# Layer 0's cross-attention: one copy of keys and queries out of PSUM by ScalarE, their two variants made by GpSimd from the copy

## The chip, the core and the metric

The kernel runs on one core of a Trainium2 chip. A core has five engines that run at the same time, each through its own queue in order: TensorE (PE, with its weight loads shown as PEld), VectorE (DVE), ScalarE (ACT), GpSimd (POOL) and SyncE (SP, which here only starts transfers). Matrix products land in PSUM, whose eight banks TensorE fills and VectorE and ScalarE read; GpSimd works in SBUF here. The metric is the time of one execution on the device in microseconds.

## What is computed

A decoder of two layers on 32 sequences of 100 tokens, width 256, each layer with self-attention, cross-attention to a context of 361 rows of width 128, and a mixture of experts. Only layer 0's cross-attention is touched:

```python
x = x + _L0_xattn_ref(_layernorm(x, axis=-1), ctx_512, L0_xattn_Wq, L0_xattn_Wkv, L0_xattn_Wo)
...
Q = (x @ Wq.T).reshape(B, xN, NUM_HEADS, HEAD_DIM)          # 16 heads of 16
KV = (z @ Wkv.T).reshape(B, zN, 2, NUM_HEADS, HEAD_DIM)
attn = jnp.einsum('bqhd,bkhd->bhqk', Q, K) * SCALE          # SCALE = 1/4
attn = jax.nn.softmax(attn, axis=-1)
O = jnp.einsum('bhqk,bkhd->bqhd', attn, V).reshape(B, xN, DIM)
return O @ Wo.T
```

## The kernel before

All of it is float32. The stage `l0_xattn` treats one sequence b in two halves c of eight heads. A projection for half c puts eight heads of 16 on 128 partitions, so that 32 partitions hold two heads, an even one (j = 0) and an odd one (j = 1). Products are made on blocks of 32 partitions, four at once; to compute the scores of one head of a block, the other head's 16 rows have to be taken out. So queries and keys are stored in two variants. `queries` (L548) projects four sequences at a time into one bank and ScalarE writes the bank to SBUF twice (L555), each time scaled per partition by `quarter`, which is 1/4 on the rows of head j and 0 on the others. `keys` (L557) does one sequence at a time: ScalarE writes it twice (L562), scaled by `own` (1 on the rows of head j, else 0) with `one` added, a single row of ones among the foreign rows. That row of ones is multiplied by the negative maximum of the scores, which `maxima` places beside the queries, so that the second, turned product already has the maximum subtracted and ScalarE can apply the exponential directly.

The loop runs over steps M = 2b + c, 64 of them and two to drain. In a step TensorE does, in an order written out by hand (`manual_schedule`): the transposes of the maxima of M-1; the scores of (M, j = 0), whose maxima VectorE takes (L590); the turned scores of (M-1, 0), whose exponentials ScalarE takes (L612); the values of M-2; the scores and turned scores for j = 1; and then the extras: `keys` for the next sequence, `queries` of the next four sequences in the odd steps 2b+1 with b mod 4 of 0 or 1, the output projection of a finished tile of 128 rows in even steps, and `vals` (L575, ScalarE copies). All banks come from one ring of eight (`bank_t`; the tag "r" falls back to it), so TensorE can run ahead of the readers by eight banks at most.

The output path of a step: ScalarE copies the values' bank (L626), VectorE swaps the halves of each 32 rows (L627), GpSimd masks (L629) and adds (L631), a step later VectorE inverts the sums (L636, held back behind the first four maxima of its step), and GpSimd multiplies into `zT` (L640), which the output projection (`out_proj`) reads. The projection in step 2b needs the product that is made in that same step.

At the start of the stage GpSimd fills the value, key and maxima buffers (L527 to L535) and makes a few index rows (L537, L539). The queues of VectorE, ScalarE and GpSimd hold their instructions in about the order in which the code above emits them. The value buffers and three key buffers are used in turn; the query tile has two buffers.

Of the kernel before, what the change touches and what calls it, by code (L numbers as in the profile page):

```python
# [9 lines left out]
F32 = mybir.dt.float32  # L10
I32 = mybir.dt.int32
U32 = mybir.dt.uint32
AF = mybir.ActivationFunctionType
ALU = mybir.AluOpType
AX = mybir.AxisListType

P = 128
NB = 32
T = 100
# [5 lines left out]
L = 361  # L25
# [96 lines left out]
class Kernel:  # L122
# [355 lines left out]
    def l0_xattn(self):  # L478
        nc, tc, a = self.nc, self.tc, self.a
        with ExitStack() as st:  # L480
# [14 lines left out]
            for h in range(H):  # L495
# [4 lines left out]
            pool = st.enter_context(tc.tile_pool(name="p0x", bufs=2))  # L500
# [11 lines left out]
            own, quarter, one = (  # L512
                cp.tile([P, 2], F32, tag=n, name=n) for n in ("own", "quarter", "one")
            )
# [13 lines left out]
            for t in vs:  # L528
                t = t.rearrange("p c (h j) e -> p c h j e", j=2)
# [18 lines left out]
            def queries(b0, c):  # L548
                if c == 0:
                    q[b0 // 4] = pool.tile([P, 2, 2, 4 * T], F32, tag="qT", name="qT")  # L550
                pm = self.bank_t()[:, : 4 * T]
                self.mm(pm, [(wq[:, k, c * P : (c + 1) * P], self.xn_of(k, b0, 4)) for k in range(NK)])
                t = q[b0 // 4]
                for j in range(2):
                    nc.scalar.activation(t[:, c, j, :], pm, AF.Copy, scale=quarter[:, j : j + 1])  # L555

            def keys(b, c):  # L557
                pm = self.bank_t()[:, :L]
                self.mm(pm, [(wk[:, c * P : (c + 1) * P], ctx[b][:, :L])])
                t = ks[b % 3]  # L560
                for j in range(2):
                    nc.scalar.activation(  # L562
                        t[:, c, j, :L], pm, AF.Identity, bias=one[:, j : j + 1], scale=own[:, j : j + 1]
                    )

            def vals(b, c0, n):
# [92 lines left out]
            def extras(b):  # L659

                k0, k1, v0, v1, o, x = [None] * 6
                if b + 1 < NB:
                    k0, k1 = (lambda: keys(b + 1, 0)), (lambda: keys(b + 1, 1))
                    v0, v1 = (lambda: vals(b + 1, 0, 2)), (lambda: vals(b + 1, 2, 1))
                if b > 1 and tile_of(b - 2) is not None:
                    o = lambda: out(tile_of(b - 2))
                b0, i = b // 4 * 4, b % 4
                if i < 2 and b0 + 4 < NB:
                    x = lambda: queries(b0 + 4, i)
                return k0, v0, o, k1, v1, x  # L670
# [11 lines left out]
            with tc.manual_schedule(engines={mybir.EngineType.PE}):  # L682
                load(0)
                load(1)
                for c in range(2):
                    queries(0, c)
                for c in range(2):
                    keys(0, c)
# [3 lines left out]
                for M in range(last + 2):  # L692
                    b, c = divmod(M, 2)
# [1526 lines left out]
```

## Time and profile before

| | us |
|---|---|
| median of 3 runs (2873.34 to 2880.9) | 2878.42 |
| profiled execution, as timed | 2879.42 |
| its span in the profile | 2877.0 |
| layer 0's cross-attention, in the span | about 521 to 1000 |
| one step of its loop | about 7.15 |
| L562, key variants by ScalarE, 128 of 128x361 | 0.679 each |
| L555, query variants by ScalarE, 32 of 128x400 | 0.598 each |
| L612, exponentials, 512 of 121x300 | 0.426 each |
| L590, maxima by VectorE, 512 of 100x361 | 0.524 each |

Busy time of an engine is the union of its instructions, so two that overlap count once; a pair of L562 takes 1.22 us from the first start to the last end. A wait "A <- B" is idle time of A that ended when B was done. "PEld" waiting means that a weight load stood still, which stops TensorE only when the matmuls already under way run out. GpSimd's durations in a profile are rough; where two instructions follow each other the distance of their starts is the better reading.

### The profile page before, as it was taken

Reading aid. Unit: us, or ns where it says so; the run is one execution under the profiler, and the core shown is the slowest. Engines: PE = TensorE matmul, PEld = TensorE weight load, DVE = VectorE, ACT = ScalarE, POOL = GpSimd, SP = SyncE. Lnnn points to the kernel's source line nnn. Section 1 sums busy time; section 2 is a strip of 40 time slices with the busy share of each in tenths; the row PEclk is TensorE's granted clock in tenths of the full one; section 3 lists DMA queues with packets and bytes.
Section 4 is the critical chain, followed back from the end, with each engine's and each line's share of the span. In section 5 each row is a group of like instructions: output and inputs, shape, how many; then the busy total and the mean of one; then the engine's idle time right before and its main releaser. Section 6 shows DMA issues by size and latency. Waiting matters only on the chain. (4 is left out here: it accounts for less than half of the span.)

```text
span 2877.0 us, 64265 instructions
## 1 busy us (share of the span) xinstructions
PE 2757.1 (96%) x24856; PEld 2132.5 (74%) x24856; DVE 1768.6 (61%) x5173; ACT 1391.3 (48%) x4210; POOL 765.2 (27%) x960
## 2 busy tenths in 40 slices
PE   8999999999999899999999999999999999999892
PEld 7888888777777657888885777777777777776572
DVE  7666766687888732222226877767676666676453
ACT  5555655677767511222223226556656566566120
POOL 3222212332222253222211330020211312223473
PEclk9999999999999899999999999999999999999996
DMA  7444333000000033655553210010000000000496
GB/s 241 137 131 165 133 140 120 22 16 16 16 16 16 17 123 121 218 203 192 195 199 93 75 39 9 7 55 17 17 15 9 15 9 14 11 10 5 121 216 188
DMA packets 133870, 241.89 MB, mean 84 GB/s; under 512 B 40715, under 2 KB 105926, under 8 KB 126769
## 3 DMA queue, kind: packets, MB, share of 16 engines
q1 hardware_dynamic: 103488, 143.53, 16.1%
q0 software_dynamic: 26784, 90.83, 9.8%
q8 instruction: 201, 3.29, 0.5%
q10 hardware_dynamic: 3280, 3.28, 0.3%
q14 instruction: 117, 0.95, 0.1%
HBM read 152.12 MB, written 111.18 MB: 92 GB/s over the span
## 5 line engine op out<-in xcount | busy, mean ns | idle before, releaser
L1816 POOL DMA_INDIRECT x_d<-xr,slot x200 | 195.0, 975 | 670.6 <-ACT eT L844 590.9
L178 PE MATMUL ps_t<-xnT,wA 128*128 128x200 f32 (+1 forms) x1608 | 323.5, 348 | 2.3 <-DMA wA<-in_wq 1.6
L178 PE MATMUL ps_t<-cT,q 128*128 128x361 f32 (+1 forms) x832 | 306.5, 471 | 0.0
L844 ACT COPY eT<-ps_t 124x384 f32<-124x384 f32 x400 | 191.2, 486 | 225.3 <-PE ps_t L843 220.2
L178 PEld LDWEIGHTS ps_t<-xnT,wA 128*128 128x128 f32 x1608 | 273.9, 192 | 31.1 <-issue 15.5
L834 ACT ACTIVATE wBx<-ps_t,m 128x361 f32<-128x361 f32 x400 | 227.4, 569 | 119.5 <-DVE m L831 109.8
L178 PE MATMUL ps_t<-xT,w 128*128 128x256 f32 (+1 forms) x1276 | 260.2, 363 | 0.7 <-ACT xT L172 0.7
L590 DVE TENSOR_REDUCE m<-ps_t 100x1 f32<-100x361 f32 x512 | 239.7, 524 | 19.2 <-PE ps_t L178 19.1
L178 PEld LDWEIGHTS ps_t<-xT,w 128*128 128x128 f32 x1276 | 223.6, 190 | 36.2 <-issue 9.3
L831 DVE TENSOR_REDUCE m<-ps_t 128x1 f32<-128x361 f32 x400 | 210.7, 527 | 59.8 <-PE ps_t L178 57.5
L843 PEld LDWEIGHTS ps_t<-ident,wBx 128*124 128x124 f32 x1200 | 150.2, 139 | 117.7 <-issue 70.7
L612 ACT ACTIVATE e<-ps_t 121x300 f32<-121x300 f32 x512 | 173.9, 426 | 122.5 <-PE ps_t L178 122.4
L384 ACT ACTIVATE e<-s,m 100x100 f32<-100x100 f32 x512 | 185.6, 364 | 66.2 <-DVE m L378 66.2
L843 PE MATMUL ps_t<-ident,wBx 128*124 128x128 f32 x1200 | 196.7, 275 | 3.6 <-DVE top L1756 2.3
L178 PE MATMUL ps_t<-wA,cT 128*124 128x512 f32 x384 | 195.6, 597 | 0.0
L388 POOL TENSOR_TENSOR e<-e,rz 100x400 f32<-100x400 f32 x128 | 109.3, 854 | 323.8 <-PE ps_t L178 208.0
L1463 DVE TENSOR_TENSOR h<-ps_t,g 128x256 f32<-128x256 f32 (+1 forms) x145 | 58.2, 402 | 188.4 <-ACT g L1462 176.0
L836 DVE TENSOR_SCALAR wBx<-wBx,sums 128x361 f32<-128x361 f32 x400 | 165.6, 414 | 9.4
L178 PEld LDWEIGHTS ps_t<-q,k 32*121 32x121 f32 x3072 | 128.3, 181 | 33.3 <-issue 7.1
L855 PEld LDWEIGHTS ps_t<-eT,v 124*64 124x64 f32 x3072 | 135.8, 138 | 15.1 <-issue 7.4
L1462 ACT ACTIVATE g<-ps_t 128x256 f32<-128x256 f32 (+1 forms) x145 | 52.9, 365 | 190.9 <-PE ps_t L178 164.2
L855 PE MATMUL ps_t<-eT,v 124*64 124x100 f32 x3072 | 140.6, 251 | 0.8 <-issue 0.7
(334 smaller groups left out, 5415.8 us busy)
## 6 DMA issues: line engine op xcount, KB each, us to landing
x_d<-fill SPq DMA_DIRECT2D x16, 1284.0 KB
we<-in_wexp SPq DMA_DIRECT2D x32, 384.0 KB
cT<-in_ctxT SPq DMA_DIRECT2D x64, 186.0 KB
xe_d<-zero SPq DMA_DIRECT2D x8, 1028.0 KB
xe<-x_d SPq DMA_DIRECT2D x24, 321.0 KB
sum<-fill SPq DMA_DIRECT2D x10, 640.0 KB
yk<-y_d SPq DMA_DIRECT2D x25, 256.0 KB
xe<-xe_d SPq DMA_DIRECT2D x24, 257.0 KB
```

What stands on the lines that cost most here:

```text
L178: self.nc.tensor.matmul(out, lhsT=l, rhs=r, start=(i == 0), stop=(i == n - 1))
L384: nc.scalar.activation(t[:, i, :], s[:, i, :], AF.Exp, bias=m[:, i : i + 1], accum_out=rz[:, i : i + 1])
L388: nc.gpsimd.tensor_tensor(t[:, h, :], t[:, h, :], self.last(rz[:, h], T), ALU.mult)
L590: got = nc.vector.tensor_reduce(m[:, j, o : o + 1], ps[r], AX.X, ALU.max, negate=True)
L612: nc.scalar.activation(t[:, r], ps[r].rearrange("p (c t) -> p c t", c=NKC), AF.Exp)
L831: self.after = nc.vector.tensor_reduce(m, ps, AX.X, ALU.max, negate=True)
L834: nc.scalar.activation(t, ps, AF.Exp, bias=m, accum_out=z)
L836: nc.vector.tensor_scalar(t, t, z, None, ALU.mult)
L843: nc.tensor.transpose(pt[:, c, :], es[n % 5][:, c * KC : (c + 1) * KC], self.ident)
L844: self.after = nc.scalar.copy(eT[:, :, o : o + P], pt)
L855: nc.tensor.matmul(pz[64 * j : 64 * j + 64, i, :], lhsT=v[:, c, h * 64 : (h + 1) * 64], rhs=eT[:, c, o : o + T], start=(c == 0), stop=(c = ...
L1816: got = nc.gpsimd.indirect_dma_start(out=self.x1_d[:, :], out_offset=bass.IndirectOffsetOnAxis(ap=slot[:, j, k : k + 1], axis=0), in_=xr[: ...
```

## The change

`queries` and `keys` take one more tile, `raw`, with three buffers. ScalarE copies the bank into it once, with no scale and no bias, and GpSimd makes both variants from it with `tensor_scalar`: one operation (multiply) for queries, two (multiply, add) for keys. What is stored in the variants is the same.

```diff
             def queries(b0, c):
...
                 t = q[b0 // 4]
+                raw = pool.tile([P, 4 * T], F32, tag="raw", name="raw", bufs=3)
+                nc.scalar.copy(raw, pm)
                 for j in range(2):
-                    nc.scalar.activation(t[:, c, j, :], pm, AF.Copy, scale=quarter[:, j : j + 1])
+                    nc.gpsimd.tensor_scalar(t[:, c, j, :], raw, quarter[:, j : j + 1], None, ALU.mult)
 
             def keys(b, c):
...
                 t = ks[b % 3]
+                raw = pool.tile([P, 4 * T], F32, tag="raw", name="raw", bufs=3)[:, :L]
+                nc.scalar.copy(raw, pm)
                 for j in range(2):
-                    nc.scalar.activation(
-                        t[:, c, j, :L], pm, AF.Identity, bias=one[:, j : j + 1], scale=own[:, j : j + 1]
+                    nc.gpsimd.tensor_scalar(
+                        t[:, c, j, :L], raw, own[:, j : j + 1], one[:, j : j + 1], ALU.mult, ALU.add
                     )
```

The order of TensorE, the loads, the buffers of the variants and everything outside these two functions stay as they are.

## The prediction

> **What bounds the kernel now.** I read the page's engine totals first, then a table of busy time for the stage that the change touches, then the waits inside it, then the rows that can price the new instructions, and last the timeline at two places. The page:
>
> ```profile
> PE 2757.1 (96%) x24856; PEld 2132.5 (74%) x24856; DVE 1768.6 (61%) x5173; ACT 1391.3 (48%) x4210; POOL 765.2 (27%) x960
> ```
>
> The cross-attention of layer 0 runs from about 521 to 1000 us. Its busy table (stretch, length, then busy us of PE, PEld, DVE, ACT, POOL, then the granted clock):
>
> ```profile
> 521.00:540.00 19.00, 18.52 (x134) 11.22 (x138) 11.11 (x34) 13.65 (x36) 7.84 (x24) 1.00 0.15 42
> 540.00:980.00 440.00, 429.67 (x7547) 330.30 (x7547) 356.64 (x970) 309.94 (x897) 128.46 (x228) 1.00 0.06 15
> 980.00:1000.00 20.00, 14.44 (x258) 11.30 (x251) 11.07 (x41) 7.79 (x21) 6.69 (x12) 0.81 0.01 2
> ```
>
> TensorE is busy 429.67 of 440 us at full clock: it is the bound, and ScalarE (310) and VectorE (357) matter only where TensorE waits for them. GpSimd idles for 70%. The waits between 540 and 980 us (who <- whom: us, times, longest):
>
> ```profile
> POOL zT L640 <- DVE zd L636: 246.1, 52, 6.9
> ...
> PEld ps_t L178 <- DVE m L590: 19.6, 85, 0.8
> ...
> PEld ps_t L178 <- ACT v L575: 7.2, 12, 1.1
> ...
> PEld ps_t L178 <- ACT k L562: 4.3, 13, 0.4
> PEld ps_t L178 <- ACT e L612: 3.3, 5, 0.9
> PEld ps_t L178 <- ACT qT L555: 2.9, 9, 0.3
> ```
>
> The reader sees two things. ScalarE holds up the weight loads for 17.7 us (19.3 with 0.8 us each of matmul waits for L575 and L612). And the largest wait of all is harmless today: GpSimd, strictly in order, stands some 5 us in every step for VectorE's reciprocal. That idle time is the room the new work must fit into.
>
> **The prices.** Removed on ScalarE: 128 activations of L562 at 679 ns and 32 of L555 at 598 ns, 106 us. Added there: 64 copies of 128x361 and 16 of 128x400; the nearest rows are copies out of PSUM of 124x384 (L844, 486 ns) and 128x400 (L409, 492 ns), so 39 us. ScalarE loses 67 us.
>
> Added on GpSimd: 128 tensor_scalars of 128x361 with two operations and 32 of 128x400 with one. The rows:
>
> ```profile
> L629 POOL TENSOR_TENSOR zs<-zs,both 128x400 f32<-128x400 f32 x64 | 66.1, 1032 | 28.9 <-DVE zs L627 28.7
> L231 POOL TENSOR_SCALAR xnx<-x_sb,mv,rstd 128x256 f32<-128x256 f32 x18 | 21.8, 1218 | 47.2 <-DVE rstd L228 36.4 <-issue 10.8
> ```
>
> L231 is the same instruction as the keys': two per-partition operands, two operations. The timeline shows it in pairs of 2.46 us, so the duration is also the spacing. Two-operand GpSimd work grows from 199 ns at 4 columns to 397 at 100 (L640): 2.06 ns a column on some 190 ns. With that start, L231 grows by (1218 - 190)/256 = 4.0 ns a column. Keys: 190 + 361x4.0 = 1.64 us. Queries: the same rate gives 1.80 us; with one operation they may cost only what two-operand work does, 190 + 400x2.06 = 1.02 us. I take 1.80, from the row with the same operation, and keep 1.02 (and 0.94 for keys at the same rate) for the low end. GpSimd gains 128x1.64 + 32x1.80 = 268 us, from 143 to 411 of the 479 us.
>
> The Trainium skill (GPSIMD Engine Reference, Engine selection) says one-input elementwise work on GpSimd runs at roughly line rate. L231 contradicts it: at its clock of 1.2 GHz 256 columns would take some 0.2 us, not 1.22. By the rule (an estimate: about 0.5 us each) the first term below would be +5, the third 0, and the sum about -9; the measurement decides.
>
> **First term, the start of the stage.** GpSimd's queue:
>
> ```profile
> 521.09 4.16 POOL L527 MEMSET v<- 121x1536 f32 x3
> ...
> 528.67 0.23 POOL L539 COPY wAn<-ids 128x25 f32<-128x25 f32 x1
> ```
>
> and TensorE's first scores:
>
> ```profile
> 526.71 1.46 PE L178 MATMUL ps_t<-k,qT 32*100 32x361 f32 x10
> ```
>
> The memsets ahead end at 528.9. Behind them now stand four query variants, then the first key variant, which the first scores need: 528.9 + 4x1.80 + 1.64 = 537.7, against 526.71. TensorE has nothing else in its hand-written order: **+11 us**. At the low prices 533.9, +7. The fourth raw tile waits for the first (three buffers) and the value copies stand behind it on ScalarE; they are needed after the scores, so that costs nothing more.
>
> **Second term, relief.** Key and query banks come free after 0.5 us instead of 1.2, and the value copies queued behind start earlier. Of the 19.3 us the waits on L562, L555 and L575 can go (15.2); those on the exps stay. Bounds 0 (the next wait, for the maxima of L590, takes over) and -19. I take **-14**, since the removed instructions are themselves what is waited for.
>
> **Third term, GpSimd's queue.** ScalarE now makes raw tiles, GpSimd waits for each, and behind a waiting or running tensor_scalar stand the three products of the output path (L629, L631, L640). L640 releases TensorE's output projection in the same step. One odd step with queries and the step behind it:
>
> ```profile
> 646.46 1.36 ACT L612 ACTIVATE e<-ps_t 121x300 f32<-121x300 f32 x4 [0.99 <-PE ps_t L178]
> ...
> 653.08 0.54 POOL L640 TENSOR_TENSOR zT<-zd 128x68 f32<-128x68 f32 x2 [4.93 <-DVE zd L636]
> ```
>
> ```profile
> 654.28 0.83 PEld L178 LDWEIGHTS ps_t<-wB,zT 128*128 128x128 f32 x4 [0.20 <-issue]
> ```
>
> After the exps the raw key copy ends near 648.3. Without queries the two key variants end at 651.6, ahead of 653.08, when the reciprocal releases L640: hidden in the 4.93 us. With queries they end at 648.3 + 2x1.64 + 2x1.80 = 655.2, L640 ends at 655.7, and the projection loads at 655.8 instead of 654.28: 1.5 us. Queries stand in 14 odd steps of the loop; in 11 of the steps that follow there is a projection: **+16 us**. Bounds: 0 at the low prices (they end at 652.2), and +30 if every such delay also makes the next reciprocal late. That reciprocal runs a step later; its product then ends some 2 us late against a slack of about as much, so I count none. The variants are needed one step (about 7 us) after they are made: no wait for scores in the loop. Loads on SyncE do not move.
>
> VectorE gets no new work. The Trainium skill (SBUF — State Buffer, Who interferes with whom) says that a VectorE instruction with two SBUF inputs contends with GpSimd's reads. L1366 shows it elsewhere (444/479/946 ns min/median/max); in this stage the 20 instructions of L1540 stayed at 164/166/177 with GpSimd at 30%. By the rule (an estimate: 50 such small instructions, half a 1.6 us product each) 40 us of VectorE's time would go, against its 83 idle; I add nothing.
>
> **Sum.** 11 - 14 + 16 = +13. The profiled execution took 2879.42 us (span 2877.0 and 2.4 around it), 1 us above the median of the three runs shown: 2892.
>
> **Rivals.**
> GpSimd is cheaper (faster). If one variant costs about 1.0 us, the start is +7, the third term 0, relief -14 to -19: 2867 to 2873, and up to 2880 if relief is half. It decides from where the four variants together take less than 5.4 us (653.08 plus the projection's 0.66 us of slack), 1.36 each; L629 and L640 speak for it in general, L231, the only long tensor_scalar on this engine, against. 0.32.
> GpSimd becomes the bound. Eight steps last 57 us and hold 8x2.2 us of products now, plus 16 key and 4 query variants; above (57 - 17.6)/20 = 1.97 us each it is full. At 2.15, 3.6 us more per eight steps, eight times, is 29 us in place of 16 + some, with a start of +12: 2910 and above. Against: 1.64 and 1.80 leave 10%. 0.10.
> Relief is nothing. The weight loads freed of ScalarE wait for L590 instead, which already stops them 85 times: 11 + 16 = +27, 2906. Against: the 12 waits on L575 reach 1.1 us, too long for L590's 0.8. 0.08.
> The forecast, 2883 to 2901, has 0.50.
>
> **How the numbers follow.** About 0.3%, 8.6 us, is what a measurement of this kernel can tell: faster is below 2870, slower above 2887. The forecast gives 0.40 slower and 0.10 same; the cheap rival 0.18 faster and 0.14 same; the other two 0.18 slower. Range: 2868 to 2910, which leaves out the cheap rival's edge and the full-queue case; the likeliest case alone has 2883 to 2901.
>
> **What would show it.** First scores near 537 rather than 527; TENSOR_SCALAR rows on POOL at 1.6 and 1.8 us; GpSimd near 85% of the stage; waits of TensorE on zT L640 of 10 us or more, on the value copies near none; ScalarE 67 us less. Variants near 1.0 us, or no wait on zT, would prove the third term wrong; waits on k or qT inside the loop would mean a delay I left out.

## The result and the profile after

The changed kernel takes 2885.17 us (median of 7 runs, 2884.41 to 2887.89) against 2879.53 us (7 runs) before. The medians differ by 5.6 us; the ratio worked out from all the runs is 1.0027, with a 95% interval of 1.0018 to 1.0036, thus 5 to 10 us slower, at the edge of what can be told apart. The forecast was 2892 in a range of 2868 to 2910, slower. The direction holds; most of the working does not. The page's first line of busy time, after:

```profile
PE 2753.7 (95%) x24856; PEld 2131.5 (74%) x24856; DVE 1769.5 (61%) x5173; ACT 1338.8 (46%) x4130; POOL 887.5 (31%) x1120
```

ScalarE lost 52 us of busy time (1391.3 to 1338.8), not 67: the forecast added up single durations, but a pair of L562 overlaps and is busy for 1.22 us, not 1.36. GpSimd gained 122 (765.2 to 887.5), not 268. GpSimd's groups between 515 and 1010 us say why (line, tiles, shape, count, busy us, mean ns, idle before):

```profile
L566 POOL TENSOR_SCALAR k<-raw,own,one 128x361 f32<-128x361 f32 x128 | 81.4, 646 | 20.5 <-ACT raw L564 17.2
L633 POOL TENSOR_TENSOR zs<-zs,both 128x400 f32<-128x400 f32 x64 | 66.1, 1032 | 15.9 <-DVE zs L631 15.7
L557 POOL TENSOR_SCALAR qT<-raw,quarter 128x400 f32<-128x400 f32 x32 | 41.2, 1296 | 0.2
```

A key variant, with two operations on 361 columns, takes 0.65 us; a query variant, with one on 400 columns, takes 1.30. The row the price was taken from (L231, two operations, 1.22 us for 256 columns) holds for neither.

**Where the time went.** The time lost stands at the start of the stage. GpSimd's timeline there, then TensorE's:

```profile
527.98 0.18 POOL L535 MEMSET k<- 128x8 f32 x3
528.10 0.16 POOL L537 IOTA ids<- 128x25 f32 x1
528.25 1.29 POOL L557 TENSOR_SCALAR qT<-raw,quarter 128x400 f32<-128x400 f32 x1
529.50 0.22 POOL L539 COPY wAn<-ids 128x25 f32<-128x25 f32 x1
529.68 3.79 POOL L557 TENSOR_SCALAR qT<-raw,quarter 128x400 f32<-128x400 f32 x3
533.47 2.52 POOL L566 TENSOR_SCALAR k<-raw,own,one 128x361 f32<-128x361 f32 x4
```

```profile
534.16 2.74 PE L178 MATMUL ps_t<-k,qT 32*100 32x361 f32 x16 [7.74 <-POOL k L566]
```

The memsets end at 528.3, four query variants and the first key variant follow, and TensorE stands still for 7.74 us, until 534.16 instead of 526.71.

The loop's length hardly moved. It is counted in all that follows from the transposes of the maxima: from the second pair (538.64 us before, 546.58 after) to the 64th (986.06 and 993.66), thus 447.42 us before and 447.08 after, in 62 steps. Many single steps agree to 0.01 us, but two things cancel in the sum: fourteen steps are shorter, by 3.2 us in all, and seven are longer, by 2.3 us in all. The seven are steps in which VectorE computes row norms (L231, the normalised rows for what follows this stage, 128x256 each) while GpSimd is busy. One of them, before and then after:

```profile
665.71 0.74 DVE L231 TENSOR_SCALAR wAn<-x_sb,mv,rstd 128x256 f32<-128x256 f32 x2
```

```profile
672.22 2.57 POOL L557 TENSOR_SCALAR qT<-raw,quarter 128x400 f32<-128x400 f32 x2
672.50 1.14 DVE L231 TENSOR_SCALAR wAn<-x_sb,mv,rstd 128x256 f32<-128x256 f32 x2
...
674.13 1.24 PE L625 MATMUL ps_t<-e,v 121*32 121x100 f32 x48 [0.52 <-DVE m L594]
```

The pair of norms takes 1.14 us instead of 0.74, the maxima behind it come later by as much, TensorE waits for them, and the step is 0.40 us longer. In each of the seven steps the norms have grown by what the step has, to 0.01 us; no other group of VectorE's instructions in the loop has grown. Before, no row norm ran at the same time as anything on GpSimd.

The waits between 551 and 991 us after:

```profile
POOL zT L644 <- DVE zd L640: 138.0, 52, 5.1
...
PEld ps_t L178 <- DVE m L594: 19.5, 69, 0.8
...
PEld ps_t L625 <- DVE m L594: 7.3, 16, 0.8
PEld ps_t L178 <- ACT v L579: 6.3, 17, 1.1
...
PEld ps_t L178 <- POOL zT L644: 0.4, 1, 0.4
```

GpSimd still waits for the reciprocal (138 us, 246 before), so its queue is not full; the wait on `zT` that was to cost 16 us is 0.4. TensorE's waits on ScalarE's key and query variants (7.2 us before) are gone; 1.1 us on GpSimd's query variants has come, and the waits on VectorE's maxima (L590 before, L594 now) have grown where the values are loaded, from 2.9 to 7.3 us.

### The profile page after: what moved, and what is told of

The parts are those of the page before. It is cut to its first block, busy times and chain, and to the rows that moved or that the text cites. A ratio compares the mean times of both kernels' runs of the same rounds, so it can differ in the third digit from the quotient of the medians.

```text
span 2885.8 us, 64443 instructions
## 1 busy us (share of the span) xinstructions
PE 2753.7 (95%) x24856; PEld 2131.5 (74%) x24856; DVE 1769.5 (61%) x5173; ACT 1338.8 (46%) x4130; POOL 887.5 (31%) x1120
## 5 line engine op out<-in xcount | busy, mean ns | idle before, releaser
L594 DVE TENSOR_REDUCE m<-ps_t 100x1 f32<-100x361 f32 x512 | 239.5, 523 | 27.9 <-PE ps_t L178 27.8
L839 DVE RECIPROCAL sums<-sums 128x1 f32<-128x1 f32 x400 | 63.7, 159 | 126.4 <-ACT wBx L838 123.3
```

The source lines that it names most:

```text
L594: got = nc.vector.tensor_reduce(m[:, j, o : o + 1], ps[r], AX.X, ALU.max, negate=True)
```

## The experiments

Twelve kernels, in three sets; each set has runs of the kernel before on its own chip (medians 2853.5, 2852.9 and 2879.4 us), so only ratios are compared across sets. Loop lengths come from one profile each, and they need care: in every profile some of the 62 steps (one to three; e5, whose probes fill the loop, is left out) ran partly at half the granted clock, which makes a step up to 1.7 us longer. The table therefore compares with the kernel before only the steps that ran at full clock in both profiles, 59 to 61 of them:

| run | loop against the kernel before, steps at full clock (us) |
|---|---|
| the change | -0.9 |
| e1, start by ScalarE | -1.1 |
| e2, loop by ScalarE | +0.1 |
| e3, one variant | -3.2 |
| e4, two operations for queries | -0.5 |
| e6, variants of the loop twice | +12.6 |
| e7, no reciprocal | -3.9 |
| e8, e1 without reciprocal | -9.4 |
| e9, e1 with a guarded start | -0.9 |
| e10, before with a guarded start | +0.3 |
| e11, e9 with VectorE relieved | -9.3 |
| e12, e10 with VectorE relieved | -2.2 |

**e1, start by ScalarE, loop by GpSimd; e2, the opposite.** The edit, for `queries` (for `keys` with b instead of b0; in e2 the condition is `b0 > 0`):

```diff
+                if b0 == 0:
+                    for j in range(2):
+                        nc.scalar.activation(t[:, c, j, :], pm, AF.Copy, scale=quarter[:, j : j + 1])
+                else:
                     raw = pool.tile([P, 4 * T], F32, tag="raw", name="raw", bufs=3)
...
```

> Queries and keys of the first sequences (b0 = 0, b = 0) made by ScalarE as before; the loop as in the changed kernel. Theory (the whole loss is the start, where GpSimd's queue delays the first scores by 7.5 us, and the loop gives back almost nothing): no change against the kernel before, -1.5 to +1 us, first scores back near 527, and step times of the loop as in both traces. Rival A (ScalarE's relief is worth 14 us in the loop and GpSimd's delay of zT takes it back): also about 0 here, but waits on zT L644 above 5 us. Rival B (relief shows once the start is repaired): -6 us or more.

> The opposite part alone: start made by GpSimd, loop by ScalarE as before. Theory: +6 to +9 us against the kernel before, the same as or 1 us above the full change, first scores near 534. Rival B (the loop gains several us): 3 us or more slower than the full change.

e2: ratio 1.0036 (1.0023 to 1.0050), first scores at 534.27, loop 447.84: the start alone carries the whole loss, at the upper end of what was expected (9.1 us between the medians). e1 was a miss: 1.0019 (1.0010 to 1.0028), where no change was expected; loop 448.50, of which 1.7 are a step at half clock. Its loss, too, is at the start, but another one. VectorE's timeline in e1:

```profile
521.57 3.27 DVE L511 CAST at<-row 128x2 f32<-128x2 int32 x1
...
525.13 2.34 DVE L517 TENSOR_SCALAR quarter<-own 128x2 f32<-128x2 f32 x1
```

and TensorE's wait that follows, in the same execution:

```profile
530.35 3.81 PE L178 MATMUL ps_t<-k,qT 32*100 32x361 f32 x16 [3.86 <-ACT k L569]
```

A cast of two columns takes 3.27 us: it lies under the GpSimd memsets of L527 (520.81 to 524.8). In the kernel before it took 0.64 and ended as the first of the three memsets did. The constants came 3.6 us later (the last, the copies of L522, ended at 527.57 instead of 523.94), and TensorE waited 3.86 us. The collision, not the loop, had to be taken away next (e9, e10).

**e3, relief alone.** ScalarE makes only the first variant, and both heads of a block read it (the sum with the maxima and the turned scores likewise):

```diff
-                for j in range(2):
+                for j in range(1):
                     nc.scalar.activation(t[:, c, j, :], pm, AF.Copy, scale=quarter[:, j : j + 1])
...
-                    self.mm(ps[r], [(q[b // 4][rows_of(r), c, j, cols], ks[b % 3][rows_of(r), c, j, :L])])
+                    self.mm(ps[r], [(q[b // 4][rows_of(r), c, 0, cols], ks[b % 3][rows_of(r), c, 0, :L])])
```

> Leaves out the second variant of queries and keys (both heads of a block read the first one), all made by ScalarE: ScalarE's 80 second activations, about 45 us of its time, are gone and GpSimd's queue is as before. Theory (ScalarE's relief is worth next to nothing, because TensorE then waits for VectorE's maxima or for itself): -2 to +0.5 us. Rival A (relief is worth about 14 us, and only GpSimd's work hides it): -8 us or more.

Ratio 0.9993 (0.9984 to 1.0002). Other values are routed after this stage, so the loop is the better witness. Its 447.89 us look like no gain, but two of its steps ran partly at half clock (stretch, length, PE, PEld, DVE, ACT, POOL, clock):

```profile
654.13:664.54 10.41, 10.16 (x123) 6.87 (x122) 5.63 (x16) 7.36 (x18) 2.19 (x4) 0.84 0.01 2
886.20:896.60 10.40, 10.15 (x123) 6.87 (x122) 5.64 (x16) 7.33 (x18) 2.17 (x4) 0.84 0.01 2
```

Both took 8.72 us in the kernel before, so 3.4 us of the loop are the clock's. At full clock e3's loop is 3.2 us shorter, and the gain lies in the same fourteen steps in which the changed kernel gained; none of e3's row norms is longer than before. So ScalarE's relief with GpSimd's queue untouched is worth 3.2 us in the loop, a little more than the 2 that the theory allowed and far less than the 8 of rival A. Of the prediction's 14 us most was not there; of what was, GpSimd's work hid 2.3 us, by slowing VectorE.

**e4, two operations for queries.**

```diff
-                    nc.gpsimd.tensor_scalar(t[:, c, j, :], raw, quarter[:, j : j + 1], None, ALU.mult)
+                    nc.gpsimd.tensor_scalar(t[:, c, j, :], raw, quarter[:, j : j + 1], 0.0, ALU.mult, ALU.add)
```

> The changed kernel with a second operation on the queries' tensor_scalar (plus 0.0). If the price on GpSimd hangs on the pair of operations and multiply-and-add is the quick one (0.65 us for 361 columns against 1.30 for the single multiply of 400), the query rows fall to about 0.70 us and the first scores come about 4 x 0.6 = 2.4 us sooner: 2 to 3 us below the full change, +3 to +4 against the kernel before. If the price hangs on columns or operands instead, the rows stay at 1.3 us or grow and the time does not fall.

Half right. The query row fell from 1296 to 603 ns by adding an operation, and the first scores came at 531.32 instead of 534.16. The ratio, 1.0023 (1.0014 to 1.0032), can't be told from the change's 1.0027. In the profiled execution one step took 10.42 us instead of 8.72, at a granted clock of 0.84 over the step, and three more of the steps with row norms grew, by 0.3 us each: both took back some of the gain.

**e5, the prices.** Four of each form, in place behind the memsets of the kernel before, on a scratch tile:

```diff
+            def probe(n, s0, s1, o0, o1):
+                for _ in range(4):
+                    nc.gpsimd.tensor_scalar(pb[:, :n], pa[:, :n], s0, s1, o0, *([o1] if o1 else []))
```

> The kernel before with a scratch tile on which GpSimd runs four tensor_scalars of each of eleven forms and four copies behind its memsets; the time means nothing, the rows do. If the pair of operations sets the price: multiply-add near 0.70 us for 400 columns with the second operand per partition or immediate, single multiply near 1.30, subtract-multiply near 1.8 (1.22 for 256, as L231). If per-partition operands set it: the form with an immediate is quicker than the one with two columns, and subtract-multiply equals multiply-add.

GpSimd's groups in five stretches that hold one form each (multiply; multiply-add, 400 then 200 columns; subtract-multiply, 400 then 256):

```profile
L548 POOL TENSOR_SCALAR pb<-pa,own 128x400 f32<-128x400 f32 x4 | 5.1, 1286 | 0.3
...
L548 POOL TENSOR_SCALAR pb<-pa,own,one 128x400 f32<-128x400 f32 x4 | 2.7, 673 | 0.4
...
L548 POOL TENSOR_SCALAR pb<-pa,own,one 128x200 f32<-128x200 f32 x4 | 2.0, 511 | 0.4
...
L548 POOL TENSOR_SCALAR pb<-pa,own,one 128x400 f32<-128x400 f32 x4 | 6.8, 1700 | 0.4
...
L548 POOL TENSOR_SCALAR pb<-pa,own,one 128x256 f32<-128x256 f32 x4 | 4.9, 1220 | 0.4
```

The pair of operations sets the price. Multiply-multiply costs 0.68 like multiply-add, multiply-subtract 1.70 like subtract-multiply, a single add, subtract or multiply 1.29, a plain copy 0.52, multiply-add with an immediate 0.60. The slope of multiply-add is (673 - 511)/200 = 0.81 ns a column, of subtract-multiply (1700 - 1220)/144 = 3.3.

**e6, every variant of the loop written twice** (start as in e1, `for j in (0, 0, 1, 1)`):

> As e1 (start by ScalarE), but GpSimd writes every variant of the loop twice, so key pairs take 2.5 us and query pairs 5.1 us of its queue. The mechanism of the prediction's third term (two key and two query variants of more than 5.4 us together hold back L644 and with it the projection): 7.6 us together, zT about 2 us late in 11 steps, +15 to +25 us against the kernel before and waits on zT of 10 us or more. Rival (the projection has room that I did not see, or GpSimd's order differs): below +5 us.

Ratio 1.0067 (1.0050 to 1.0084), about 19 us, of which 6 are the start, as in e1 (second transposes at 544.73 us instead of 538.64); loop 460.64, 13.2 us longer. The waits between 552 and 990 us:

```profile
PEld ps_t L178 <- POOL zT L654: 12.3, 11, 1.5
...
PE ps_t L178 <- POOL zT L654: 7.9, 11, 1.1
```

Eleven places, as the prediction counted them, and at most 13.2/11 = 1.2 us each, where 2 were expected; part of it is row norms, which are longer here too. So the third term's mechanism is real and its threshold lies between 3.9 us (two key and two query variants after the change: 2x0.65 + 2x1.30) and 7.6.

**e7 and e8, without VectorE's reciprocal**, in the kernel before and in e1 (in both the line and the dependence on it are removed):

```diff
-                got = nc.vector.reciprocal(zs[:, 1, :], zs[:, 1, :])
```

> The kernel before without VectorE's reciprocal L636 (the output is multiplied by the sums instead of divided): 64 x 0.78 = 50 us of VectorE's time and its place between two groups of maxima are gone. If VectorE's maxima share in the bound of the loop: -8 us or more. If TensorE's own sequence is all that bounds it: -3 us or less.

> As e1 and without the reciprocal, left out as in e7. If the waits on L590 swallowed ScalarE's relief, the relief shows now that VectorE has room: 4 us or more below e7. If the waits on ScalarE were never stops of TensorE: within 2 us of e7.

The output that follows is another one and with it the experts' load, so their times (ratio 1.0324 both) say nothing here. The loops are 445.23 us in e7 and 438.71 in e8. At full clock 50 us less of VectorE's time is worth 3.9 us with ScalarE's variants, a miss of the 8 expected. With GpSimd's variants (e8) the loop is 9.4 us shorter than before, and over the steps at full clock in both 5.3 below e7, as expected for e8. Relief of either engine alone is worth 3 to 4 us, of both together 9, though in e8 the row norms are still slowed.

**e9 and e10, the guarded start**: e1, and the kernel before, with the memsets held until VectorE's constants are written.

```diff
-                nc.gpsimd.memset(t, 0.0)
+                got = nc.gpsimd.memset(t, 0.0)
+                self.depend(got, [setup.ins], "behind VectorE's constants")
```

Here `setup` is the last of these constants, the copy of L522.

> As e1, and GpSimd's memsets at the start wait for VectorE's last constant, so that VectorE's small set-up instructions can't stand behind them (in e1's profile L511 took 3.27 us instead of 0.64 and the first scores came at 530.4 instead of 526.7). Theory (e1's remaining loss is that collision, the loop is neutral): equal to e10 within 2 us, step times as in the changed kernel, L511 below 0.3 us. Rival (the loop with GpSimd's variants costs 3 to 5 us by itself): 3 us or more above e10.

> The kernel before with the same wait at the start; control for e9. Theory: within 2 us of the kernel before, perhaps 1 us faster, since the constants come sooner and the value buffers later.

L511 takes 0.14 us in both. e9: ratio 0.9991 (0.9982 to 1.0000), loop 446.78; e10: 1.0005 (0.9996 to 1.0014), loop 450.04 with one step at 10.41 us. With the start repaired the change costs nothing; at full clock its loop is 0.9 us shorter than that of the kernel before and 1.3 shorter than e10's. Between the medians e9 lies 3.6 us below e10 (2876.78 and 2880.38), where at most 2 were expected. In the profiles 1.9 us of this lies ahead of the stage, where the two kernels have the same code: VectorE's first set-up instruction (L508) starts at 519.50 in e9 and at 521.37 in e10.

**e11 and e12, VectorE relieved**: as e9 with e4's queries, and as e10; in both the stage's row norms go to GpSimd and its transposed copies to ScalarE (`turn_act` is 1 within the stage).

```diff
-        self.evac(self.xnT[:, :, f * P : (f + n) * P], pt)
+        self.evac(self.xnT[:, :, f * P : (f + n) * P], pt, getattr(self, "turn_act", 2))
...
-                xn = self.norm_rows(f, n, rows=self.rows, after=self.after)
+                xn = self.norm_rows(f, n, rows=self.rows, after=self.after, eng=nc.gpsimd)
```

> As e9, with the queries' second operation (0.60 us each on GpSimd) and some 17 us of VectorE's time moved away: the 30 row norms of this stage (0.41 us each) to GpSimd, the seven transposed copies (0.69 us) to ScalarE. Theory (TensorE's remaining waits are for VectorE, and ScalarE's relief shows when VectorE is relieved): 3 to 8 us below the kernel before and below e12. Rival (relief of either engine is worth nothing): within 2 us of e9 and e10.

> The kernel before with the guarded start and the same relief of VectorE as in e11, but with the variants still made by ScalarE. Theory: between e10 and e11, 1 to 4 us below e10. Rival: as e10.

e11 is faster than both kernels: 2869.61 us, ratio 0.9967 (0.9956 to 0.9978), loop 438.71. e12, the same without the change: 0.9997 (0.9988 to 1.0006), loop 445.82. The change, with the queries' second operation, is worth 7.1 us of the loop where VectorE is lighter; e8 against e7 gives 5.3 at full clock. In e11 the row norms are also out of the way of GpSimd's variants, and none of the seven steps is longer: up to 2.3 of the 7.1 us can be that, which no run separates from VectorE's lighter load. Busy times in the same 440 us of e12 and of e11 (PE, PEld, DVE, ACT, POOL):

```profile
545.00:985.00 440.00, 431.11 (x7533) 331.08 (x7528) 345.12 (x938) 314.26 (x905) 163.21 (x258) 1.00 0.06 14
```

```profile
545.00:985.00 440.00, 427.37 (x7625) 331.43 (x7620) 345.00 (x954) 268.17 (x837) 256.81 (x409) 0.99 0.06 14
```

More matmuls fit into the same time (7625 against 7533) at an equal load of VectorE, with ScalarE at 268 instead of 314.

## Why the prediction was right, and where it was wrong

**First term, the start (+11).** Right in kind and place. It was +7.5: four query variants at 1.29 instead of 1.80, a key variant at 0.65 instead of 1.64, and the copy of L539 between them. e2 shows that this term alone carries the loss.

**Second term, relief (-14).** The step that failed. I read 15.2 us of weight-load waits named after ScalarE as time that would come back; e3 gives 3.2 of it. A load of the turned scores in the step that I walked through, in the kernel before, in the changed kernel and in e3, each behind the sum of queries and maxima (L600, L604) that it needs:

```profile
649.49 0.37 DVE L600 TENSOR_TENSOR q<-ps_t,qT 128x200 f32<-128x200 f32 x1 [1.59 <-PE ps_t L598]
...
649.97 1.07 PEld L178 LDWEIGHTS ps_t<-q,k 32*121 32x121 f32 x24 [0.33 <-ACT qT L555]
```

```profile
656.27 0.37 DVE L604 TENSOR_TENSOR q<-ps_t,qT 128x200 f32<-128x200 f32 x1 [1.59 <-PE ps_t L602]
...
656.76 0.86 PEld L178 LDWEIGHTS ps_t<-q,k 32*121 32x121 f32 x24 [0.33 <-ACT v L579]
```

```profile
647.41 0.37 DVE L600 TENSOR_TENSOR q<-ps_t,qT 128x200 f32<-128x200 f32 x1 [1.59 <-PE ps_t L598]
647.89 0.86 PEld L178 LDWEIGHTS ps_t<-q,k 32*121 32x121 f32 x24 [0.33 <-ACT v L575]
```

It stood for 0.33 us each time, whatever the name, and each time VectorE's sum had ended 0.11 or 0.12 us before it: the name was that of the last semaphore, the wait was for VectorE. Where TensorE did get ahead, it met VectorE again: in that step its values began 1.75 us after the scores before and 1.55 after, and the next keys 4.39 us after them in both, behind the maxima. Of my rivals "relief is nothing", at 0.08 the least likely, is the nearest on this term; e8 and e11 show that more of the relief appears once VectorE is lighter.

**Third term, GpSimd's queue (+16).** Wrong in size: 0. The single wait of 0.4 us on `zT` is there in e3 too, whose queue on GpSimd is as before. The threshold, 5.4 us for the four variants, is not contradicted (3.9 us held nothing back, and e6's 7.6 held the projection back in the 11 places), but the price taken, 6.9, was above it. "The row with the same operation" was the wrong rule: L231's instruction on GpSimd has the same name but subtracts first, and e5 prices that pair at 2.5 times multiply-add (1.70 against 0.67 us for 400 columns). The rule of the Trainium skill that I set aside for it (GPSIMD Engine Reference, Engine selection: one-input work at roughly line rate) agrees with multiply-add, whose 0.81 ns a column is about one cycle of the 1.2 GHz that the page gives, and not with a single operation or a pair with subtract.

**VectorE (put at nothing).** "VectorE gets no new work" is so, but it was slowed: GpSimd's variants ran into its row norms, which the two rows that I looked at (L1366, L1540) did not include, and the loop lost 2.3 us by it.

The terms as the runs show them are +7.5, -3.2, 0 and +2.3, together +6.6, near the 5.6 us between the medians. The forecast of +13 lies not far off because its errors (3.5 too much for the start, 10.8 too much for the relief, 13.7 too much for GpSimd's queue and VectorE) largely cancel, which was luck. The rival with cheap GpSimd was nearer in the prices and forecast a gain, wrong by the same missing relief.

**What stays open.** Why in e1 the cast stood through three memsets and before through one wasn't tried, nor a run that moves the row norms alone. e9's gain can't be told from nothing. Why the clock is halved in single steps of the loop, and whether the same steps are hit in the executions that were not profiled, was not seen.

## What to carry to other kernels

A wait that the profile names after an engine is only worth what the next wait on the same instruction leaves: test it by relieving that engine alone before counting the whole sum, and compare only steps that ran at the same granted clock: two halved stretches hid e3's 3.2 us. Price an instruction by its exact operations, not by its name and shape, and when work moves to an idle engine look first at what that engine's queue holds at the start of the stage, where nothing covers it, and then at what its longer queue runs beside on the other engines.

## What the runs showed of the hardware

- On GpSimd a tensor_scalar with two operations can be twice as fast as with one: 128x400 at 0.67 us for multiply-add, 0.68 for multiply-multiply, 1.29 for multiply alone, 1.70 for pairs of a multiply and a subtract.
- At the start of the stage the granted clock fell to half for some 7 us where TensorE had stood still for 3.2 us (e6), 3.9 (e1), 5.0 (e4) or 7.7 (the changed kernel), and not where it had not (before, e9). In the changed kernel the first scores were 7.45 us late and the second transposes 7.94 (stretch, length, PE, PEld, DVE, ACT, POOL, clock):

```profile
526.00:534.00 8.00, 0.42 (x2) 0.01 (x1) 0.00 (x0) 1.58 (x7) 8.00 (x21) 0.80 0.09 24
534.00:539.00 5.00, 4.84 (x23) 2.54 (x23) 3.29 (x8) 0.46 (x1) 2.19 (x5) 0.63 0.00 0
539.00:544.00 5.00, 4.60 (x66) 3.12 (x65) 4.19 (x10) 3.42 (x9) 1.06 (x2) 1.00 0.01 3
```

- It was also halved for 3.4 us inside single steps of the loop in which TensorE was busy nearly throughout (e3's two rows above: 10.16 of 10.41 us), at a cost of 1.7 us each.
- A pair of VectorE's row norms (128x256, one tensor input) took 0.74 us with GpSimd idle and up to 1.14 us beside its tensor_scalars.
- A VectorE cast of two columns took 0.14 us alone and 3.27 (e1) or 4.41 (e5, e6) while GpSimd's memsets ran; VectorE's set-up instructions of one column took 0.14 to 0.15 us beside memsets of the same line (e1). The Trainium skill (SBUF — State Buffer, Who interferes with whom) says that casts, copies and tensor_scalars of VectorE in a two-port mode and GpSimd instructions shut each other out for a whole instruction. These rows agree in that the cast ended with a memset: with the first of three before, with the third in e1, so there it stood through more than one. Which mode it ran in, no run shows.
